# The last two groups of an attention pooling: second buffers, an interleaved order, and unread matmuls

## Chip, core and metric

The kernel runs on one core of a Trainium2 chip. The metric is device time in microseconds (us): the median over several runs of one program. The core's engines work side by side, each through its own queue of instructions in order: TensorE (PE in the profile; its weight loads, PEld, are a row of their own), VectorE (DVE), ScalarE (ACT), GpSimd (POOL) and SyncE (SP), which here only issues DMAs. TensorE writes into PSUM, eight banks of 128 x 512 float32, and the other engines read from there.

## The reference, cut to what matters

The input x has 64 sequences of 64 tokens with 256 features (4096 tokens). Two residual blocks follow each other: a linear attention with a rotated input, and a pooling that feeds a feed-forward network (FFN) with quantized operands.

```python
x = x + attn(cond(x, delta_t, amplitudes, frequencies), W_qkv, W_o, log_gamma)
x = x + ffn(cond2(x, W1, b1, v, prompt_type_ids), clip_x, clip_down, w_gate, w_up, w_down)

def cond2(hidden, W1, b1, v, ids):             # the pooling
    attn_in = jnp.tanh(jnp.einsum('bsd,da->bsa', hidden, W1) + b1)
    scores = jnp.einsum('bsa,a->bs', attn_in, v)
    ...                                        # a mask per prompt type
    p = jax.nn.softmax(jnp.where(mask, scores[:, None, :], NEG_INF), axis=-1)
    cnt = jnp.sum(mask, axis=-1).astype(hidden.dtype)
    return jnp.einsum('bjl,bld->bjd', p, hidden) / cnt[..., None]

def act_fake_quant(x, clip_factor):            # inside ffn, on its input and on h
    scale = jax.nn.sigmoid(clip_factor) * jnp.max(jnp.abs(x)) / 127.0
    return jnp.clip(round(x / scale), -128.0, 127.0) * scale

# ffn: h = silu(xq @ gate.T) * (xq @ up.T), quantized again, times down
```

What matters for the change: the scale of the FFN's input is one number, from the largest absolute value of the whole pooled tensor. No token can be quantized, and no matmul of the FFN can start, before the last group of tokens is pooled.

## The kernel before, in words

**Tiling.** The 4096 tokens are cut into eight groups (g = 0 to 7) of 512: four tiles (GT) of 128 tokens on the 128 partitions, so a tile holds two sequences. x stays in SBUF as xg[g]. `u` names a pair of tiles (256 tokens); `both` is (0, 1), `u0` is (0,) and `u1` is (1,).

**Stages.** A loop (L848 to L899) lays three groups over each other: keys, queries and values of group p, attention of group a = p - 1, pooling of group q = p - 2. The tail (L902 to L959) ends attention of group 7 (`a`) and pooling of group 6 (`q`) and 7; `a` is taken in its two halves u0 and u1. Then comes the FFN: quantizing, gate and up in four passes of 1024 tokens, a second maximum, and the down projection with the output.

**Order.** In the attention part TensorE, ScalarE, VectorE and GpSimd each run their instructions in the order in which the Python code calls them (`manual_schedule`, L120). In the FFN that holds for ScalarE, VectorE and GpSimd; TensorE's order there is laid by the planner.

**The steps of the pooling**, in the order in which a group goes through them:
- `hidden` (L437): matmuls by W1 into a bank `pa`, then on ScalarE the tanh into the tile `th` (L453).
- `token_scores` (L456): the matmul of th by v into a bank `psr` (L459).
- `softmax_exp` (L462): VectorE adds the mask to psr and writes `ms` (L470), takes the maximum (L477) and subtracts it (L478); ScalarE applies exp (L481). For group 6 the subtraction is GpSimd's.
- `softmax_div` (L483): sum (L488), product with the count (L491), reciprocal (L492), product with ms (L493, for group 6 on GpSimd).
- `weights_transposed` (L497): TensorE transposes ms into a bank `pp` (L503); ScalarE (`by_act`, L507) or VectorE (L509) copies it into the tile `pT`.
- `pooling` (L512): small matmuls of 64 x 64 from pT and x into two banks `pl` (L526): 64 instructions in the trace for a group, 32 for a half.
- `pooled_copies` (L535): ScalarE copies the two banks into `pooled` (L539).
- `pooled_maxima` (L541): VectorE reduces the same two banks (`from_banks`) to columns of `xam` (L546). The program orders two engines that touch one PSUM bank as they are written: in the tail each reduction waits for ScalarE's copy of its bank.

**What follows the pooling.** `warm` (L956) applies Silu to one column, so that its activation table is loaded before the FFN; the profile shows an ACT_TABLE_LOAD there. `act_scale` (L97) reduces xam (L100), transposes the result through the bank `pmx` (L103), reduces again (L104), and forms the scale and its inverse rx (L105, L108). `quantize_tokens` of groups 0 and 1 (L1001 on ScalarE, L999 and L1002 on VectorE) makes the first `xq`, in four pieces (two halves of the features, two groups). In `gate_up`, TensorE's first gate tile pg needs all four (L1049); among the matmuls of pg and pu in the planner's order, its last is the eighth. ScalarE then applies Silu (gate, L1060), copies pu for GpSimd (L1066) and makes the next int8 tokens (L1011).

**Buffers.** A tile of a pool with `bufs=1` is one place in SBUF: its next writer waits until the last reader of the previous tile is done. `th`, `ms` and `pT` are such tiles; the pool's default is two (L112). In PSUM `bank` (L140) takes the next of four banks of the ring `ps`, or, while `spare[0]` is set, of the ring `ps_sc`, also four, which the attention's scores use before. A bank, too, is given again only when its readers are done.

The tail is written out by hand; from L927 on, the calls are these:

```python
residual(a, 1); softmax_div(q, by=nc.gpsimd); transposed_pair(a, 1)
hidden(a, u0); hidden(a, u1); token_scores(a, u0); token_scores(a, u1)
spare[0] = True
weights_transposed(q, by_act=True); pooling(q)
spare[0] = False
...
```

Of the kernel before, what the change touches and what calls it, by code (L numbers as in the profile page):

```python
# [9 lines left out]
F32 = mybir.dt.float32  # L10
# [8 lines left out]
P = 128  # L19
# [8 lines left out]
def adaln_attn_ffn(  # L28
# [20 lines left out]
    nc = tc.nc  # L49
    B, S, D = x.shape  # L50
# [7 lines left out]
    GT = 4  # L58
# [13 lines left out]
    xg = [  # L72
        const.tile([P, GT, D], F32, tag=f"x{g}", name=f"x{g}") for g in range(NG)
    ]
# [16 lines left out]
    wgT = const.tile([P, 2, FF], BF16, name="wgT")  # L91
# [5 lines left out]
    def act_scale(cols, k, scale, inv, pt):  # L97

        mx = const.tile([P, 1], F32, name=f"mx{k}")
        nc.vector.tensor_reduce(mx, cols, AX.X, ALU.max)  # L100

        allmx = const.tile([P, 1], F32, name=f"allmx{k}")
        nc.tensor.transpose(pt, mx.to_broadcast([P, P]), ident)  # L103
        nc.vector.tensor_reduce(allmx, pt, AX.X, ALU.max)  # L104
        nc.vector.tensor_scalar(  # L105
            scale, allmx, csig[:, k : k + 1], 1.0 / QMAX, ALU.mult, ALU.mult
        )
        nc.vector.reciprocal(inv, scale)  # L108


    with ExitStack() as actx:
        pool = actx.enter_context(tc.tile_pool(name="att", bufs=2))  # L112
# [22 lines left out]
        xam = big.tile([P, 2 * NG + 2], F32, name="xam")  # L135


        spare = [False]

        def bank(name):  # L140
            if spare[0]:
                t = ps_sc.tile([P, 2, 2, 2 * S], F32, tag="sc", name=name)
                return t.rearrange("p i f c -> p (i f c)")
            return ps.tile([P, 512], F32, tag="bank", name=name)


        T = {}
# [284 lines left out]
        both = (0, 1)  # L432
# [4 lines left out]
        def hidden(g, us=both):  # L437

            pu, _ = span(us)
            pa = bank(f"pa_{g}_{us[0]}")[:, 0 : len(us) * P]  # L440
            x2v = T.pop(("x2T", g, us)).rearrange("p c (u k l) -> p c k u l", k=2, l=P)
            for kc in range(2):
                for k in range(2):
                    nc.tensor.matmul(  # L444
                        pa[k * A : (k + 1) * A, :],
                        w1s[:, kc, :],
                        x2v[:, kc, k, pu],
                        start=(kc == 0),
                        stop=(kc == 1),
                    )  # L450
            th = pool.tile([P, 2 * P], F32, tag="th", name=f"th_{g}_{us[0]}", bufs=1)
            th = th[:, 0 : len(us) * P]
            nc.scalar.activation(th, pa, AF.Tanh, bias=b1s)  # L453
            T["th", g, us] = th

        def token_scores(g, us=both):  # L456

            psr = bank(f"psr_{g}_{us[0]}")[:, 0 : len(us) * P]
            nc.tensor.matmul(psr, vb, T.pop(("th", g, us)), start=True, stop=True)  # L459
            T["psr", g, us] = psr  # L460

        def softmax_exp(g, us=both, by=nc.vector):  # L462
            _, pt = span(us)
            n = 2 * len(us)
            ms = T.get(("ms", g))
            if ms is None:
                ms = pool.tile([P, GT, S], F32, tag="ms", name=f"ms_{g}", bufs=1)
                T["ms", g] = ms
            ms = ms[:, pt]
            nc.vector.tensor_tensor(  # L470
                ms,
                T.pop(("psr", g, us)).rearrange("p (t l) -> p t l", l=S),
                T["bias", g][:, pt],
                ALU.add,
            )
            mx = pool.tile([P, GT], F32, tag="mx", name=f"mx_{g}_{us[0]}")[:, 0:n]
            nc.vector.tensor_reduce(mx, ms, AX.X, ALU.max)  # L477
            by.tensor_tensor(  # L478
                ms, ms, mx.unsqueeze(2).to_broadcast([P, n, S]), ALU.subtract
            )  # L480
            nc.scalar.activation(ms, ms, AF.Exp)  # L481

        def softmax_div(g, us=both, by=nc.vector):  # L483
            _, pt = span(us)
            n = 2 * len(us)
            ms = T["ms", g][:, pt]
            ssum = pool.tile([P, GT], F32, tag="ssum", name=f"ssum_{g}_{us[0]}")[:, 0:n]
            nc.vector.tensor_reduce(ssum, ms, AX.X, ALU.add)  # L488
            rs = pool.tile([P, GT], F32, tag="rs", name=f"rs_{g}_{us[0]}")[:, 0:n]
            c = g * GT + 2 * us[0]  # L490
            nc.vector.tensor_mul(rs, ssum, cnt[:, c : c + n])  # L491
            nc.vector.reciprocal(rs, rs)  # L492
            by.tensor_tensor(  # L493
                ms, ms, rs.unsqueeze(2).to_broadcast([P, n, S]), ALU.mult
            )

        def weights_transposed(g, us=both, by_act=False):  # L497

            _, pt = span(us)
            pp = bank(f"pp_{g}_{us[0]}")[:, 0 : len(us) * P]  # L500
            msv = T["ms", g].rearrange("p (u k) l -> p u (k l)", k=2)
            for i, u in enumerate(us):
                nc.tensor.transpose(pp[:, i * P : (i + 1) * P], msv[:, u, :], ident)  # L503
            pT = pool.tile([P, GT, S], F32, tag="pT", name=f"pT_{g}_{us[0]}", bufs=1)
            pTv = pT[:, pt].rearrange("p t j -> p (t j)")
            if by_act:
                nc.scalar.copy(pTv, pp)  # L507
            else:
                nc.vector.tensor_copy(pTv, pp)  # L509
            T["pT", g, us] = pT  # L510

        def pooling(g, us=both):  # L512

            xs, pT = xg[g], T.pop(("pT", g, us))
            _, pt = span(us)
            pls = [
                bank(f"pl_{g}_{us[0]}_{k}").rearrange("p (c t j) -> p c t j", c=2, j=S)
                for k in range(2)
            ]
            for kc in range(2):  # L520
                for t in range(2 * us[0], 2 * us[-1] + 2):
                    for dh in range(2):
                        cols = slice(kc * P + dh * 64, kc * P + (dh + 1) * 64)
                        for k in range(2):
                            half = slice(k * S, (k + 1) * S)
                            nc.tensor.matmul(  # L526
                                pls[k][dh * 64 : (dh + 1) * 64, kc, t, :],
                                xs[half, t, cols],
                                pT[half, t, :],
                                start=True,  # L530
                                stop=True,
                            )
            T["pl", g, us] = pls

        def pooled_copies(g, us=both):  # L535
            pls, pt = T["pl", g, us], span(us)[1]
            pv = pooled[g].rearrange("p c (t k j) -> p c t k j", k=2, j=S)
            for k in range(2):
                nc.scalar.copy(pv[:, :, pt, k, :], pls[k][:, :, pt])  # L539

        def pooled_maxima(g, us=both, from_banks=False):  # L541
            pls, pt = T.pop(("pl", g, us)), span(us)[1]
            pv = pooled[g].rearrange("p c (t k j) -> p c t k j", k=2, j=S)
            for k in range(2):
                col = 2 * g + k if us[0] == 0 else 2 * NG + k
                nc.vector.tensor_reduce(  # L546
                    xam[:, col : col + 1],
                    pls[k][:, :, pt] if from_banks else pv[:, :, pt, k, :],
                    AX.XYZ,
                    ALU.max,  # L550
                    apply_absolute_value=True,
                )
# [349 lines left out]
        a, q = NG - 1, NG - 2  # L902
# [27 lines left out]
        hidden(a, u0)  # L930
        hidden(a, u1)
        token_scores(a, u0)
        token_scores(a, u1)
        spare[0] = True
        weights_transposed(q, by_act=True)
        pooling(q)
        spare[0] = False
        softmax_exp(a, u0)
        softmax_exp(a, u1)
        softmax_div(a, u0)  # L940
        pooled_copies(q)
        weights_transposed(a, u0, by_act=True)
        softmax_div(a, u1)
        weights_transposed(a, u1)
        pooled_maxima(q, from_banks=True)
        pooling(a, u0)
        spare[0] = True
        pooling(a, u1)
        pooled_copies(a, u0)
        pooled_maxima(a, u0, from_banks=True)  # L950
        pooled_copies(a, u1)
        pooled_maxima(a, u1, from_banks=True)
        spare[0] = False

        warm = const.tile([P, 1], F32, name="warm")
        nc.scalar.activation(warm, hm[:, 0:1], AF.Silu)  # L956
        sx = const.tile([P, 1], F32, name="sx")
        rx = const.tile([P, 1], F32, name="rx")
        act_scale(xam, 0, sx, rx, bank("pmx_0")[:, 0:P])  # L959


    with ExitStack() as fctx:
# [234 lines left out]
```

## Time and profile before

| | us |
|---|---|
| median of 3 runs | 325.21 (324.16 to 326.14) |
| the profiled execution | 324.3 |
| its span, first to last instruction | 322.6 |
| busy: PE, DVE, ACT, POOL | 277.9, 233.3, 197.7, 87.9 |
| mean granted TensorE clock, share of full | 0.963 |

The profile is of one execution. Its times count from the start of the span. "Busy" is the time in which an engine has an instruction under way; the granted clock is the share of full speed that the chip gives to TensorE. The stages around the change in that execution:

| us from the start | what happens |
|---|---|
| 217.7 to 220.9 | last attention output matmuls (po, L399) |
| 220.7 to 224.2 | x of group 7 transposed, hidden, first token scores |
| 224.9 to 226.9 | weights of group 6 transposed and copied, group 6 pooled |
| 225.4 to 229.0 | softmax of group 7 on VectorE, both halves |
| 228.3 to 231.8 | weights of group 7 transposed and copied, group 7 pooled |
| 230.5 to 233.1 | six maxima on VectorE |
| 233.1 to 234.6 | the scale of the FFN's input |
| 234.7 to 237.5 | first tokens quantized |
| 235.8 to 283.4 | gate and up matmuls |
| 289.2 on | quantizing of h and the down projection; its matmuls begin at 290.6 |

How it is read: an engine's share of the span says little here, since each stage has another limit. The useful views are the chain of waits that ended last, the timeline of the stretch, and the table of busy time and clock by stretches.

### The profile page before, as it was taken

The page shows a single profiled execution, that of the slowest core. Times are in us where ns is not written, and L with a number is a line of the kernel's source. Part 1 is how long each engine was busy: PE and PEld are TensorE (multiplying, and loading weights), DVE is VectorE, ACT ScalarE, POOL GpSimd, SP SyncE. Part 2 cuts the span into 40 slices and gives each one's busy share as a digit, 9 for nine tenths or more (in the row PEclk, how much of TensorE's full clock was granted, in tenths as well). Part 3 has the DMA queues.
Part 4 walks back from the last instruction along what each step waited for, and adds up shares of the span by engine and source line. Part 5 has one row for each costly group of instructions (what it writes and reads, how often), then busy time and mean ns, then how long its engine had stood idle before and what let it go on. Part 6 is the DMA issues. An engine that isn't in the chain of part 4 may idle for free.

```text
span 322.6 us, 8705 instructions
## 1 busy us (share of the span) xinstructions
PE 277.9 (86%) x3762; PEld 196.9 (61%) x3766; DVE 233.3 (72%) x503; ACT 197.7 (61%) x300; POOL 87.9 (27%) x81
## 2 busy tenths in 40 slices
PE   0499999999989999999999999998478999819990
PEld 0286768758848857865875885876323433307880
DVE  6679785876997696597397378374737889977881
ACT  1566448586774755647358457363549998829930
POOL 0051240510140060045002100053008888602540
PEclk9999999999999999999999999999759999966997
DMA  5592620101100200200100010020000000000998
GB/s 150 137 327 64 207 82 20 50 2 35 35 0 2 69 2 0 69 2 4 44 25 2 13 56 2 2 70 0 3 2 0 1 0 2 0 0 0 160 192 170
DMA packets 16789, 16.15 MB, mean 50 GB/s; under 512 B 2160, under 2 KB 16496, under 8 KB 16752
## 3 DMA queue, kind: packets, MB, share of 16 engines
q1 hardware_dynamic: 12480, 11.83, 11.7%
q0 software_dynamic: 3696, 3.67, 7.5%
q8 instruction: 29, 0.48, 0.6%
q10 hardware_dynamic: 576, 0.11, 0.2%
q14 instruction: 8, 0.07, 0.1%
HBM read 7.74 MB, written 7.86 MB: 48 GB/s over the span
## 4 chain that ended last, share of the span: by engine, by line
PE 56%; DVE 22%; ACT 13%; issue 3%; DMA 3%; ACTq 0%; DVEq 0%
PE pv L215 9%; PE po L399 9%; PE pdn L1127 7%; PE pk L215 5%; PE psc L330 5%; PE py L372 4%; ACT gate L1060 4%; DVE hT L1069 3%; ACT L245 3%; DVE at L355 3%; DMA afb<-n_L_cond_amplitudes_dram 3%; PE pa L444 3%; PE pl L526 2%; PE pkT L277 2%; DVE xam L546 2%
## 5 line engine op out<-in xcount | busy, mean ns | idle before, releaser
L355 DVE TENSOR_TENSOR at<-psc,gam 128x512 f32<-128x512 f32 x62 | 38.4, 681 | 13.6 <-PE psc L330 13.6
L161 POOL TENSOR_TENSOR ys<-x,cs 128x1024 f32<-128x1024 f32 x7 | 13.8, 1968 | 110.8 <-DVE xr L175 88.9
L1067 POOL TENSOR_TENSOR hT<-gate,up 128x1024 f32<-128x1024 f32 x11 | 26.0, 2360 | 27.2 <-ACT up L1066 27.2
L399 PE MATMUL po<-woT,yT 128*128 128x256 f32 x128 | 30.7, 384 | 2.7 <-DVE kn L261 2.7
L1049 PE MATMUL pg<-xq,wgT 128*128 128x512 bf16 (+1 forms) x94 | 26.3, 397 | 4.3 <-ACT gate L1060 2.0
L215 PE MATMUL pv<-wvT,xT 128*128 128x256 f32 x128 | 29.8, 386 | 0.1
L290 PE MATMUL pq<-xT,wqT 128*128 128x512 f32 x64 | 29.5, 604 | 0.0
L215 PE MATMUL pk<-wkT,xT 128*128 128x256 f32 x128 | 29.2, 381 | 0.2 <-ACT xT L205 0.2
L1060 ACT ACTIVATE gate<-pg,wsx 128x1024 f32<-128x1024 f32 (+1 forms) x25 | 24.5, 1024 | 6.3 <-PE pg L1049 3.8
L399 PEld LDWEIGHTS po<-woT,yT 128*128 128x128 f32 x128 | 23.3, 190 | 8.2 <-DVE kn L261 5.1
L1024 DVE TENSOR_REDUCE ham<-hT 128x1 f32<-128x1024 f32 (+1 forms) x25 | 26.0, 1082 | 0.7 <-POOL hT L1067 0.7
L215 PEld LDWEIGHTS pv<-wvT,xT 128*128 128x128 f32 x128 | 23.7, 190 | 4.6 <-issue 1.4
L215 PEld LDWEIGHTS pk<-wkT,xT 128*128 128x128 f32 x128 | 23.5, 190 | 3.7 <-ACT xT L205 0.9
L1049 PE MATMUL pu<-xq,wuT 128*128 128x512 bf16 (+1 forms) x94 | 24.0, 391 | 1.6 <-DVE hT L1069 1.4
L1127 PE MATMUL pdn<-wdT,hq 128*128 128x256 bf16 x192 | 23.3, 289 | 2.3 <-DVE hq L1002 2.3
L1001 ACT ACTIVATE hq<-hT,rh 128x2560 int16<-128x2560 f32 (+4 forms) x10 | 20.1, 2095 | 6.3 <-DVE rh L108 6.3
L1127 PEld LDWEIGHTS <-hq 128*128 128x128 bf16 x192 | 19.9, 104 | 5.8 <-issue 2.6
L298 ACT ACTIVATE qbd<-pq,hm 128x512 f32<-128x512 f32 x32 | 20.1, 679 | 4.9 <-PE pq L290 4.8
L1069 DVE SCALAR_TENSOR_TENSOR hT<-pu,wsx,gate 128x1024 f32<-128x1024 f32 (+1 forms) x14 | 14.5, 1051 | 9.9 <-ACT gate L1060 9.9
L330 PE MATMUL psc<-qbd,kT 32*64 32x128 f32 x1024 | 20.2, 279 | 0.5 <-ACT kT L280 0.3
L290 PEld LDWEIGHTS pq<-xT,wqT 128*128 128x128 f32 x64 | 11.5, 190 | 14.0 <-issue 11.5
L388 ACT ACTIVATE yT<-py,hm 128x256 f32<-128x256 f32 x32 | 13.4, 470 | 10.8 <-PE py L372 10.8
(190 smaller groups left out, 524.6 us busy)
## 6 DMA issues: line engine op xcount, KB each, us to landing
x<-in_x_dram SPq DMA_DIRECT2D x8, 512.0 KB, 6.4
out_dram<-x SPq DMA_DIRECT2D x7, 512.0 KB, 3.9
out_dram<-x POOLq DMA_DIRECT2D x7, 512.0 KB, 7.6
wq_nat<-in_L_attn_W_qkv_dram SPq DMA_DIRECT2D x3, 256.0 KB, 8.7
wnat_d<-in_L_ffn_w_down_dram SPq DMA_DIRECT2D x1, 704.0 KB, 6.1
wnat<-in_L_ffn_w_gate_dram SPq DMA_DIRECT2D x1, 640.0 KB, 4.5
wnat<-in_L_ffn_w_up_dram SPq DMA_DIRECT2D x1, 640.0 KB, 5.7
out_dram<-x SPq DMA_DIRECT2D x2, 256.0 KB, 6.3
```

The source lines that it names most:

```text
L215: nc.tensor.matmul(pk[:, i * D : (i + 1) * D], xT[:, kc, t * P : (t + 1) * P], w[:, kc, :], start=(kc == 0), stop=(kc == 1),)
L290: nc.tensor.matmul(pq, wqT[:, kc, hf * P : (hf + 1) * P], xT[:, kc, :], start=(kc == 0), stop=(kc == 1),)
L298: nc.scalar.activation(qbd[:, hf, :, k, :], pq.rearrange("p (b s) -> p b s", s=S), AF.Copy, scale=hm[:, k : k + 1],)
L330: nc.tensor.matmul(banks[p][k * S : (k + 1) * S, i, hf, :], kT[rows, hf, b * S : (b + 1) * S], qbd[rows, hf, b].rearrange("p k t -> p (k t)"),
L355: nc.vector.tensor_tensor(dst, scores, by, ALU.mult)
L399: nc.tensor.matmul(po[:, i * D : (i + 1) * D], yT[:, i, hf].rearrange("p k t -> p (k t)"), woT[:, hf, :], start=(hf == 0), stop=(hf == 1),)
L1024: nc.vector.tensor_reduce(ham[:, nham : nham + 1], h, AX.XY, ALU.max, apply_absolute_value=True)
L1049: nc.tensor.matmul(dst[:, k, :] if wide else dst[k * LAST : (k + 1) * LAST, 0, :], w[:, kc, c * P : min((c + 1) * P, FF)], xq[:, kc, g * G ...
L1060: nc.scalar.activation(gate[:, ns], pg[:, ns], AF.Silu, scale=wsx[:, 0, c : c + 1])
L1067: nc.gpsimd.tensor_tensor(h, gate, up, ALU.mult)
L1069: nc.vector.scalar_tensor_tensor(h, pu[:, ns], wsx[:, 1, c : c + 1], gate[:, ns], ALU.mult, ALU.mult)
L1127: nc.tensor.matmul(pdn[:, i, :], hq[j][:, NF if last else 2 * c + k, tok], wdT[:, c + k if last else c, :], start=(c == 0), stop=(c == NC ...
```

## The change

It touches the buffers of three tiles, four helpers and the tail's order:
- `th`, `ms` and `pT` have two buffers each.
- A new helper `busy(dst, n)` issues n matmuls of the gate weights by themselves (128 x 512, bf16) into a bank that nothing reads. It is called with 3 after the pooling of group 6, with 4 after the pooling of group 7, and with 6 after the transpose in `act_scale`.
- `pooling` can do the two halves of the features (kcs) one at a time, and `pooled_copies` the two banks (ks).
- In the tail, the transposes of group 6's weights stand between the two halves' token scores of group 7; the copies of group 6 and the pooling of group 7's first half are cut in two and interleaved with the transposes; the second half's weights are copied by ScalarE and not by VectorE; the maxima of group 6 stand before the last pooling; the Silu activation `warm` stands before group 7's copies and not behind its maxima. Some banks come from the other ring.

```diff
+    def busy(dst, n):
+
+        for _ in range(n):
+            nc.tensor.matmul(
+                dst, wgT[:, 0, 0:P], wgT[:, 0, 0 : dst.shape[-1]], start=True, stop=True
+            )
...
-            th = pool.tile([P, 2 * P], F32, tag="th", name=f"th_{g}_{us[0]}", bufs=1)
+            th = pool.tile([P, 2 * P], F32, tag="th", name=f"th_{g}_{us[0]}")
...
-                ms = pool.tile([P, GT, S], F32, tag="ms", name=f"ms_{g}", bufs=1)
+                ms = pool.tile([P, GT, S], F32, tag="ms", name=f"ms_{g}")
...
-            pT = pool.tile([P, GT, S], F32, tag="pT", name=f"pT_{g}_{us[0]}", bufs=1)
+            pT = pool.tile([P, GT, S], F32, tag="pT", name=f"pT_{g}_{us[0]}")
...
-        def pooling(g, us=both):
+        def pooling(g, us=both, kcs=(0, 1)):
...
-            for kc in range(2):
+            if 0 in kcs:
+                T["pl", g, us] = [
+                    bank(f"pl_{g}_{us[0]}_{k}").rearrange("p (c t j) -> p c t j", c=2, j=S)
+                    for k in range(2)
+                ]
+            pls = T["pl", g, us]
+            for kc in kcs:
...
-        def pooled_copies(g, us=both):
+        def pooled_copies(g, us=both, ks=(0, 1)):
             pls, pt = T["pl", g, us], span(us)[1]
             pv = pooled[g].rearrange("p c (t k j) -> p c t k j", k=2, j=S)
-            for k in range(2):
+            for k in ks:
                 nc.scalar.copy(pv[:, :, pt, k, :], pls[k][:, :, pt])
...
         token_scores(a, u0)
+        spare[0] = True
+        weights_transposed(q, by_act=True)
+        spare[0] = False
         token_scores(a, u1)
         spare[0] = True
-        weights_transposed(q, by_act=True)
         pooling(q)
         spare[0] = False
         softmax_exp(a, u0)
         softmax_exp(a, u1)
+        busy(bank("idle_q"), 3)
         softmax_div(a, u0)
-        pooled_copies(q)
+        pooled_copies(q, ks=(0,))
+        spare[0] = True
         weights_transposed(a, u0, by_act=True)
+        spare[0] = False
         softmax_div(a, u1)
-        weights_transposed(a, u1)
+        pooling(a, u0, (0,))
+        pooled_copies(q, ks=(1,))
+        spare[0] = True
+        weights_transposed(a, u1, by_act=True)
+        spare[0] = False
+        pooling(a, u0, (1,))
         pooled_maxima(q, from_banks=True)
-        pooling(a, u0)
-        spare[0] = True
         pooling(a, u1)
-        pooled_copies(a, u0)
-        pooled_maxima(a, u0, from_banks=True)
-        pooled_copies(a, u1)
-        pooled_maxima(a, u1, from_banks=True)
-        spare[0] = False

         warm = const.tile([P, 1], F32, name="warm")
         nc.scalar.activation(warm, hm[:, 0:1], AF.Silu)
+        for us in (u0, u1):
+            pooled_copies(a, us)
+            pooled_maxima(a, us, from_banks=True)
+        spare[0] = True
+        pmx0, idle = bank("pmx_0")[:, 0:P], bank("idle_a")
+        spare[0] = False
+        busy(idle, 4)
         sx = const.tile([P, 1], F32, name="sx")
         rx = const.tile([P, 1], F32, name="rx")
-        act_scale(xam, 0, sx, rx, bank("pmx_0")[:, 0:P])
+        act_scale(xam, 0, sx, rx, pmx0)
+        busy(idle, 6)
```

## The prediction

> **What bounds the kernel now.** The page comes first: it says whether one engine bounds the whole or several stages have limits of their own. Its section 2 (40 slices of 8.07 us) shows a kernel that TensorE fills until slice 28. There PE and its granted clock fall together, while no other engine fills up:
>
> ```profile
> PE   0499999999989999999999999998478999819990
> ...
> ACT  1566448586774755647358457363549998829930
> ...
> PEclk9999999999999999999999999999759999966997
> ```
>
> Slices 28 and 29 (225.8 to 241.9 us) are the end of pooling and the start of gate/up: the place of the change. The chain of waits there says whose end counts: VectorE's softmax of the last group, its copy of the weights, six maxima, the scale, then eight gate/up matmuls, then ScalarE's first gate.
>
> ```profile
> 225.42 0.30 DVE ms L470
> ...
> 229.19 0.30 PE pp L503
> 229.48 0.69 PE pl L526 x32
> ...
> 230.27 0.29 DVE pT L509
> 230.56 2.53 DVE xam L546 x6
> ...
> 233.12 0.18 DVE mx L100
> ...
> 239.47 1.11 ACT gate L1060
> ```
>
> From that gate on ScalarE runs without a gap to 248.7 us, so what is gained before 239.47 is gained at the end. The timeline names each hold (start, duration, instruction; in brackets the idle time before it and what ended it):
>
> ```profile
> 224.18 0.37 ACT L453 ACTIVATE th<-pa,b1s 128x128 f32<-128x128 f32 x1 [0.78 <-PE psr L459]
> ...
> 225.42 0.29 DVE L470 TENSOR_TENSOR ms<-psr,bias 128x128 f32<-128x128 f32 x1 [3.06 <-PE pp L503]
> ...
> 227.45 1.05 ACT L539 COPY pooled_b<-pl 128x512 f32<-128x512 f32 x2
> ...
> 230.27 0.29 DVE L509 COPY pT<-pp 128x128 f32<-128x128 f32 x1 [1.23 <-PE pl L526]
> ...
> 231.80 0.65 ACT L539 COPY pooled_b<-pl 128x256 f32<-128x256 f32 x2 [0.99 <-PE pl L526]
> ...
> 232.46 1.28 ACT L956 ACT_TABLE_LOAD   x1
> ...
> 233.35 0.47 PE L103 MATMUL pmx<-ident,mx 128*128 128x128 f32 x1 [1.60 <-DVE mx L100]
> ...
> 235.79 0.61 PE L1049 MATMUL pg<-xq,wgT 128*128 128x512 bf16 x1 [1.97 <-DVE xq L1002]
> ```
>
> Three holds are single buffers: the second tanh waits until the first is read (L453), the last group's scores until the group before is transposed out of the same ms (L470), the second weights until the first pooling has read pT (L509). Last, TensorE's busy time and clock by stretch. I laid the stretches back from 230.31, where the granted clock falls, in the 3.41 us that divides the distances between its turns (230.31, 240.55, 284.96, 295.2: 10.24 is three, 54.65 sixteen):
>
> ```profile
> 223.48:226.90 3.42, 2.50 (x76) 1.79 (x71) 1.36 (x5) 1.05 (x3) 0.00 (x0) 1.00 0.00 0
> 226.90:230.31 3.41, 1.26 (x38) 0.83 (x34) 1.96 (x10) 1.69 (x5) 0.00 (x0) 1.00 0.02 5
> 230.31:233.72 3.41, 1.50 (x33) 1.12 (x33) 2.95 (x8) 2.40 (x5) 0.00 (x0) 0.50 0.01 2
> ...
> 237.14:240.55 3.41, 3.41 (x10) 1.21 (x9) 0.39 (x2) 1.08 (x2) 0.00 (x0) 0.50 0.02 5
> ```
>
> The second number is PE's busy time, the third from the end the clock. After a stretch with 1.26 of 3.41 us busy (37%) the clock is halved; after one with 2.50 (73%) it was not. At half clock gate/up matmuls start 0.427 us apart (236.62, 237.04, 237.47), later 0.216.
>
> **The change, step by step.**
>
> *Second ms, th.* Scores of the first half end at 224.15 (L453's release at 224.18), so VectorE adds the mask at 224.19 instead of 225.42: -1.23. The second half's scores must be there by 225.04, when VectorE comes to them. The second tanh no longer waits: its input ends at 223.73, it ends at 224.15. The moved transposes of group 6 run in the 0.33 to 0.71 us after the first scores' start at 223.66 (their distance now: 224.60 to 224.93 and 225.31), to 224.37; the second scores then take 224.2 to 224.74. In time. VectorE's fourteen small softmax steps follow one another without a stop now (225.42 to 229.04), so the whole stretch moves by 1.23 and ends at 227.81.
>
> *ScalarE's queue in the new order.* Group 6's weights 224.41 to 224.78, its pooling on PE (1.16) to 225.99. Exponentials to 226.32. First copy of group 6 (0.57) to 226.87. First half's weights: transposed 227.04 to 227.34 (0.15 and 0.30 behind the division, as now), copied 227.43 to 227.70. Second copy of group 6 to 228.24. Second half's weights, now by ScalarE into a second pT, transposed to 228.35, copied to 228.67. PE's last pooling (0.69 for 32 at full clock) ends at 229.41. The 1.23 that VectorE waited at L509 is gone, and VectorE takes group 6's two maxima (0.60 apart) from 227.84 to 229.12.
>
> *The moved table load.* This is the step that takes most of it back. The Silu activation now stands ahead of group 7's four copies: 1.28 of load and 0.20, from 228.68 to 230.18. The four copies (0.37 each, 0.27 apart as at 230.16) end at 230.55, 230.82, 231.1 and 231.37. Each maximum of group 7 waits for the copy of its bank, as it does now; VectorE, free at 229.12, stands still until 230.59. Four maxima 0.33 apart, the last 0.42, end at 232.00; the reduction of xam starts at 232.03 instead of 233.12: **-1.09**. Without that wait it would be 230.47 (-2.65).
>
> By the Trainium skill (ScalarE: Activation LUTs, Rules for kernel authors) a switch of tables is to be budgeted at about 2.7 us, which would put the maxima some 1.2 us later and leave nothing of the -1.09. The trace has the load at 1.28 us, the next instruction 0.02 us behind it, and the copy before it ending 0.01 us ahead.
>
> *Unread matmuls.* 128x512 bf16, 0.216 apart at full clock. Three after group 6's pooling: done by 226.6, before PE is next wanted at 227.04. Four after the last pooling: 229.41 to about 230.3, before the maximum's transpose at 232.26. Six behind that transpose: to 233.9; the first gate/up matmul is not ready before 234.54. Cover 0.4, 1.9 and 0.6 us: cost nothing. At half clock the six take 2.56 and would hold the gate matmuls by 0.6.
>
> *What a full clock is worth.* The transpose of the maximum: 0.30 (like pp) in place of 0.47: **-0.16**. Quantizing then starts at 233.44 (234.69 - 1.25). The gate's last matmul of the first eight ran from 238.75 to 239.38; its last input (the last L1002, 237.09 + 0.29) was there at 237.38, so at full clock it would have ended at 237.38 + 0.05 + 0.38 = 237.81: **-1.57**. Gate at 236.65 instead of 239.47.
>
> *At nothing.* Second buffers in the loop over groups: the waits there are of other kinds; only the tail's instructions show such a wait. Reading th, ms, pT at other addresses: no row prices it; from the spread of equal forms (0.415 to 0.416 for maxima) I take 0, +-0.1. The halves of group 6's copies and group 7's pooling: same instructions in another order. No DMA is moved.
>
> *Sum:* 1.09 + 0.16 + 1.57 = **-2.82 us**. The profiled execution took 324.3 (span 322.6): 321.5, span 319.8. Against the median 325.21: **322.4**.
>
> *Unknown: does the clock hold?* PE is idle from 230.3 to 232.26. A stretch of 3.41 us holds, by where it begins, 1.45 to 1.64 us of work at the worst (42 to 48%). Between the rows 37% (fell) and 73% (held), it is nearer to the one that fell; but much of that one was short 64-wide matmuls in small pieces, and here it is dense 512-wide ones. I take that it holds, with little lead. If it falls, by the beat of this trace at 233.72, the gate matmuls start at 234.54, 0.427 apart, until 237.14, and the eighth ends at 237.7: gate 237.8, -1.67. If it falls at 232.4, the six take half clock to 235.1, the clock is back at 235.8, gate 237.4: -2.07.
>
> The Trainium skill (TensorE: Matmul & The Clock Gate, the table on why this matters) asks only that no idle gap between bursts exceeds about 3 us. By that rule the clock holds here, with -2.82. The trace does not agree with it: the clock fell at 230.31 with no idle gap over 1.4 us in the stretch before.
>
> **The rivals.**
>
> *A, forecast:* 322.4. Chance 0.45.
>
> *B, the clock falls in the new gap:* 325.21 - 1.67 to - 2.07, 323.3. For it: 42% is close to 37%. Against: above. 0.33.
>
> *C, the other side: the transposes of group 6 block TensorE's queue.* Moved ahead of the second scores, they wait for GpSimd's division L493. Its row ends at 223.11, but spans on POOL are rough, and today's transposes prove it done only by 224.82. From 224.2 on it decides. At 224.9 the second scores come at 225.74 and VectorE's second half at 225.78 (+0.74), second weights at 229.4, maxima at 232.7 (-0.33 in place of -1.09); the gap on PE makes the clock fall, the six unread matmuls hold the gate by 0.6, and all eight at half clock put it at 239.76: +0.3, 325.5. Against it: no wait of PE for POOL in the list of waits. 0.06.
>
> *D, the maxima don't wait for the copies:* -2.65 - 0.16 - 1.57 = -4.4, 320.8. No maximum in the trace begins before the copy of its bank ends, though VectorE was busy anyway. 0.05.
>
> *E, the load holds ScalarE longer than its row.* The widest bound is all the time from the last copy to the quantizing, 232.45 to 234.69: 2.24 for 1.50. Then xam is at 232.77, the clock falls, the unread six run into the gate: 238.6 to 239.7, 325.21 - 0.9 to + 0.2, 324.8. 0.06. The table rule above is of this kind.
>
> *F, the change does not do what it says:* the freed waits return as others at the same places: 325.2. 0.05.
>
> **The numbers.** This kernel's runs (324.16 to 326.14) tell no change within about 0.5%, 1.6 us. A is faster beyond that but for noise (0.93), B in 0.6, D surely, C, E and F mostly neither: faster 0.68, same 0.26, slower 0.06. The second fall of the clock, before the down projection (4.6 us at half clock, 290.6 to 295.2), meets the beat elsewhere after a shift: 2.3 us lost now, between 1.4 and 3.4 then, so -0.9 to +1.1 on any case. Range: A and B with that, from 322.4 - 1.4 to 323.3 + 1.9, reaching C and E: 321.0 to 325.2.
>
> **What would show it.** L470 of group 7 at about 224.2 with no wait for pp; L509 gone; the table load at about 228.7, directly ahead of four copies; an idle VectorE of some 1.4 us ahead of the first 128x256 maximum, ended by ScalarE; reduction at 232.0; clock 1.00 through 240, gate matmuls 0.216 apart, first gate at 236.7. I am wrong if the maxima run on without that gap (D), if the clock is 0.5 at the first gate matmul (B), or if PE waits for POOL at L503 (C).

## The result, and the profile after

| | before | changed |
|---|---|---|
| median (range), us | 324.76 (324.16 to 326.14), 4 runs | 321.57 (320.23 to 322.07), 4 runs |
| ratio, 95% interval | | 0.9889 (0.9844 to 0.9935) |
| span of the profiled execution | 322.6 | 320.2 |
| mean granted clock | 0.963 | 0.98 |

A later series of both on another occasion gave 321.48 for 325.36, ratio 0.9891 (0.9869 to 0.9914).

The same rows of the page, for the changed kernel (slices of 8.0 us, counted from 0): PE shows 8 at slice 28, where it had 4, and still 7 at slice 29; its clock is full through slice 34.

```profile
PE   0399999999999999998999999999878999919990
...
PEclk9999999999999999999999999999999999976998
```

Two profiled executions do not begin alike: the changed one reaches the tail 0.94 us later (the chain of the changed one begins with the load of another small tensor, 9.44 us for 8.51). I therefore count from the start of the last attention residual (second x<-po,x: 220.93 before, 221.87 after) to the start of the first gate, and call this **the stretch**. It is 239.47 - 220.93 = 18.54 us before and 237.69 - 221.87 = **15.82** after: -2.72.

The chain of waits of the changed kernel in the stretch (start, duration, instruction):

```profile
225.18 0.30 DVE ms L477
...
229.51 0.27 ACT pT L514
...
229.79 1.28 ACT L967
...
231.29 0.27 ACT pooled_b L547
...
231.58 1.43 DVE xam L554 x4
233.03 0.18 DVE mx L100
...
233.26 0.34 PE pmx L103
...
237.69 1.11 ACT gate L1079
```

In these traces only ScalarE and VectorE read PSUM banks, and the chain passes through both now: from the second half's weights (L514) into the table load (L967), the copies (L547), all on ScalarE, and only then the four maxima on VectorE. Before, it stayed on VectorE from the mask addition to xam, but for the transposes and the pooling. The timeline of the same moments:

```profile
225.18 0.29 DVE L477 TENSOR_TENSOR ms<-psr,bias 128x128 f32<-128x128 f32 x1 [1.89 <-PE psr L466]
...
228.86 1.28 DVE L554 TENSOR_REDUCE xam<-pl 128x1 f32<-128x512 f32 x2
...
229.79 1.28 ACT L967 ACT_TABLE_LOAD   x1
...
231.08 0.20 ACT L967 ACTIVATE warm<-hm 128x1 f32<-128x1 f32 x1
...
231.58 1.42 DVE L554 TENSOR_REDUCE xam<-pl 128x1 f32<-128x256 f32 x4 [1.43 <-ACT pooled_b L547]
...
233.26 0.32 PE L103 MATMUL pmx<-ident,mx 128*128 128x128 f32 x1 [1.77 <-DVE mx L100]
...
235.58 0.39 PE L1068 MATMUL pg<-xq,wgT 128*128 128x512 bf16 x1 [0.70 <-DVE xq L1021]
```

The mask addition waits for its scores (psr) and no longer for the transposes of the group before (pp). VectorE does the maxima of group 6 and then stands still for 1.43 us, released by ScalarE's copy. TensorE, too, waits 0.70 us for tokens ahead of the first gate matmul: the six unread matmuls were done. Its busy time (second number) and clock (third from the end), in stretches of the same 3.41 us, laid back from the next fall of the clock at 283.44:

```profile
228.83:232.24 3.41, 2.64 (x69) 1.52 (x67) 1.98 (x5) 3.00 (x8) 0.00 (x0) 1.00 0.01 2
232.24:235.66 3.42, 1.70 (x8) 0.73 (x9) 2.03 (x9) 1.31 (x3) 0.00 (x0) 1.00 0.02 5
```

The clock held after 1.70 us of work in 3.41. The same kernel, run once more (e9 below), shows nearly the least work that such a stretch can hold here: its gap of 1.77 us lay whole within one stretch, which leaves 1.64 us of work, and the clock held there too.

```profile
230.28:233.69 3.41, 1.64 (x8) 0.64 (x7) 2.26 (x8) 1.31 (x5) 0.00 (x0) 1.00 0.02 5
233.69:237.10 3.41, 2.71 (x13) 1.18 (x13) 2.02 (x7) 1.53 (x3) 0.00 (x0) 1.00 0.00 0
```

### The profile page after: what moved, and what is told of

The parts are those of the page before. It is cut to its first block, busy times and chain, and to the rows that moved or that the text cites. A ratio compares the mean times of both kernels' runs of the same rounds, so it can differ in the third digit from the quotient of the medians.

```text
span 320.2 us, 8727 instructions
## 1 busy us (share of the span) xinstructions
PE 279.4 (87%) x3779; PEld 197.8 (62%) x3779; DVE 232.9 (73%) x502; ACT 197.7 (62%) x301; POOL 87.5 (27%) x81
## 4 chain that ended last, share of the span: by engine, by line
PE 56%; DVE 21%; ACT 14%; DMA 3%; issue 3%; ACTq 1%; DVEq 0%
PE pv L222 9%; PE po L406 9%; PE pdn L1146 7%; PE pk L222 6%; PE psc L337 5%; PE py L379 4%; ACT gate L1079 4%; DMA lgb<-in_L_attn_log_gamma_dram 3%; DVE hT L1088 3%; ACT L252 3%; DVE at L362 3%; PE pa L451 3%; PE pl L535 2%; ACT x L1030 2%; PE pkT L284 2%
## 5 line engine op out<-in xcount | busy, mean ns | idle before, releaser
L1068 PE MATMUL pg<-xq,wgT 128*128 128x512 bf16 (+1 forms) x96 | 25.1, 381 | 3.4 <-ACT gate L1079 2.7
L238 ACT ACTIVATE sq<-pk 128x512 f32<-128x512 f32 x16 | 9.6, 597 | 17.1 <-PE pk L222 17.1
```

What stands on the lines that cost most here:

```text
L1068: nc.tensor.matmul(dst[:, k, :] if wide else dst[k * LAST : (k + 1) * LAST, 0, :], w[:, kc, c * P : min((c + 1) * P, FF)], xq[:, kc, g * G ...
```

## The experiments

All stretches are from one profiled execution each; over thirteen profiles the time from the first gate to the last output sum on VectorE stays within 74.9 to 75.4 us, so a difference in the stretch goes through to that sum. Medians lie beside runs of the kernel before in the same series. The gain of a median differs from that of its stretch by -0.3 us (e1) to +1.3 us (e7), so one stretch tells a median to about 1 us and no better.

| run | stretch, us | xam reduced, us into it | median, us (before) | ratio, 95% |
|---|---|---|---|---|
| before | 18.54 | 12.19 | | |
| changed | 15.82 | 11.16 | 321.57 (324.76) | 0.9844 to 0.9935 |
| e1 no unread matmuls | 17.55 | 11.17 | 324.61 (325.28) | 0.9954 to 0.9998 |
| e2 table load last | 14.55 | 9.90 | 320.33 (325.28) | 0.9819 to 0.9878 |
| e3 maxima first | 14.29 | 9.63 | 320.88 (325.28) | 0.983 to 0.989 |
| e4 buffers only | 16.72 | 10.40 | 323.11 (325.28) | 0.9905 to 0.9959 |
| e5 unread matmuls only | 16.80 | 12.17 | 323.70 (325.49) | 0.9919 to 0.9964 |
| e8 buffers and unread, old order | 15.06 | 10.40 | 321.64 (325.49) | 0.9837 to 0.9913 |
| e6 twelve instead of six | 15.83 | 11.17 | one run, 323.21 | |
| e7 without the four | 17.85 | 11.16 | 323.52 (325.49) | 0.9913 to 0.9961 |

**e1: are the unread matmuls what holds the clock?**

```diff
-        busy(bank("idle_q"), 3)
...
-        busy(idle, 4)
...
-        busy(idle, 6)
```

> The changed kernel without its thirteen unread matmuls; all else as there. Read on the stretch from the start of the last attention residual (x, second one) to the first gate: 18.54 us before, 15.82 after. Theory (they hold the clock): the reduction of xam starts where it does now (11.2 us into the stretch), but of the 3.41 us in which it is transposed only some 0.4 us are busy, so the granted clock falls to 0.5 ahead of the first gate/up matmul, these come 0.427 us apart, and the gate is some 1.6 us later: stretch about 17.4, time about 323.2. Rival (the clock held because the new order leaves TensorE no long gap): clock 1.00 at the first gate matmul without them, stretch 15.8, time 321.6.

Stretch 17.55, 1.73 longer, and xam is reduced at the same place (11.17). The clock falls at 232.18 and is back at 239.0. Its timeline:

```profile
232.92 0.48 PE L103 MATMUL pmx<-ident,mx 128*128 128x128 f32 x1 [2.74 <-DVE mx L100]
...
237.08 1.06 PE L1065 MATMUL pg<-xq,wgT 128*128 128x512 bf16 x2
...
239.08 1.12 ACT L1076 ACTIVATE gate<-pg,wsx 128x1024 f32<-128x1024 f32 x1 [3.46 <-PE pg L1065]
```

The maximum's transpose takes 0.48 again and two gate matmuls 1.06, as before the change. The rival, that the new order alone holds the clock, is out. The median is a miss, 1.4 above the 323.2 expected: its ten executions have mean clocks of 0.960 to 0.970, and the profiled one is among the two highest; what the others lost, no profile shows.

**e2 and e3: does the early table load take part of the gain back?** e2 moves the load behind copies and maxima; e3 leaves it and lets the maxima read the banks first.

```diff
-        warm = const.tile([P, 1], F32, name="warm")
-        nc.scalar.activation(warm, hm[:, 0:1], AF.Silu)
         for us in (u0, u1):
             pooled_copies(a, us)
             pooled_maxima(a, us, from_banks=True)
+        warm = const.tile([P, 1], F32, name="warm")
+        nc.scalar.activation(warm, hm[:, 0:1], AF.Silu)
```

> The changed kernel with the Silu activation, and so its table load, put back behind the copies and maxima of the last group. Theory (the load ahead of the copies holds the maxima): VectorE's 1.43 us of waiting ahead of the first 128x256 maximum shrinks to about 0.2, the reduction of xam comes 1.2 us sooner, the load runs behind the copies in time that ScalarE has free; stretch about 14.6, time about 320.4. Rival (the load is hidden where it is, the maxima wait for the last pooling): stretch 15.8 and time 321.6, or later if the load now holds the first quantizing.

```diff
-            pls, pt = T.pop(("pl", g, us)), span(us)[1]
+            pls, pt = T["pl", g, us], span(us)[1]
...
         for us in (u0, u1):
-            pooled_copies(a, us)
             pooled_maxima(a, us, from_banks=True)
+        for us in (u0, u1):
+            pooled_copies(a, us)
```

> The changed kernel with the load left where it is, and the last group's four maxima written ahead of its four copies, so that the copies wait for the maxima. Theory (it is the order of the two readers of a bank that makes the load count): the maxima follow those of the group before with at most 0.2 us of waiting, xam is reduced 1.4 to 1.5 us sooner, the copies end before the scale is known; stretch about 14.3, time about 320.1. Rival (the maxima wait for something else than the copies): stretch 15.8, time 321.6.

Stretches 14.55 and 14.29: 1.27 and 1.53 shorter than the change, for the expected 1.2 and 1.4 to 1.5. In e2 the load ends at 231.80 and `warm` at 232.01, ahead of the inverse scale that ScalarE needs next (232.37). The timeline of e3:

```profile
228.77 2.61 DVE L554 TENSOR_REDUCE xam<-pl 128x1 f32<-128x512 f32 x6
...
229.70 1.28 ACT L967 ACT_TABLE_LOAD   x1
...
231.11 1.18 ACT L547 COPY pooled_b<-pl 128x256 f32<-128x256 f32 x4
...
231.41 0.17 DVE L100 TENSOR_REDUCE mx<-xam 128x1 f32<-128x18 f32 x1
```

Six maxima in one go, while the same load runs at the same place; the copies end at 232.29, ahead of the inverse scale (232.74). The load costs only because the maxima stand behind copies that stand behind it. Both versions are faster than the kernel before and, in the stretch, than the change.

**e4, e5, e8: the parts by themselves**, added to the kernel before.

```diff
# e4 and e8
-            th = pool.tile([P, 2 * P], F32, tag="th", name=f"th_{g}_{us[0]}", bufs=1)
+            th = pool.tile([P, 2 * P], F32, tag="th", name=f"th_{g}_{us[0]}")
...
# e5 and e8
         softmax_exp(a, u1)
+        busy(bank("idle_q"), 3)
...
         pooled_maxima(a, u1, from_banks=True)
+        idle = bank("idle_a")
         spare[0] = False
+        busy(idle, 4)
...
         act_scale(xam, 0, sx, rx, bank("pmx_0")[:, 0:P])
+        busy(idle, 6)
```

> The kernel before with second buffers for th, ms and pT and nothing else: old order, no unread matmuls, load behind the copies. Theory (the buffers give the early start, the order and the load take a part back, the unread matmuls give the clock): first mask addition of the last group 1.2 us sooner, the wait ahead of the second weights' copy down from 1.23 to about 0.5, xam reduced 1.8 us sooner than before (more than the whole change's 1.0), clock 0.5 at the gate matmuls; stretch 16.7, time about 323.0. Rival (the buffers alone free nothing, since the old order makes the same instructions wait for others): stretch 18.5, time 324.8.

> The kernel before with the thirteen unread matmuls alone (three after the pooling of the group next to last, four after the last pooling, six behind the maximum's transpose): single buffers, old order. Theory (they are worth the clock and no more): xam is reduced where it was, 12.2 us into the stretch, the clock is 1.00 at the first gate matmul, the transpose of the maximum takes 0.32 instead of 0.47, and the gate is 1.7 us sooner: stretch 16.8 for 18.54, time about 323.3. Rival (without the new order TensorE has longer gaps, which thirteen matmuls don't fill): the clock still falls, the six then take 2.56 us and hold the first gate matmuls by about 0.6: stretch 18.5 to 19.2.

> The kernel before with the second buffers and the unread matmuls, in the old order with the table load behind the last copies. Theory (the three parts add up: buffers 1.82, unread 1.73, the new order with its early load a loss of 0.83): stretch 15.0, shorter than the whole change's 15.82; time about 321.0. Rival (the new order is what lets buffers and unread matmuls work together): stretch at least 15.8.

e4 gives 16.72 (16.7 expected), e5 16.80 (16.8), e8 15.06 (15.0). In e4 the wait ahead of the second weights' copy is 0.48:

```profile
228.35 0.29 DVE L509 COPY pT<-pp 128x128 f32<-128x128 f32 x1 [0.48 <-PE pp L503]
```

There xam comes 1.79 us sooner than before, where the whole change brings 1.03. So the parts are: buffers -1.82, unread matmuls -1.74, and the new order with its early load +0.76 on top of both (15.82 - 15.06). The order itself, with the load out of the way, is a gain: e2 against e8, 14.55 to 15.06, -0.51.

**e6: do more unread matmuls cost?**

```diff
-        busy(idle, 6)
+        busy(idle, 12)
```

> The changed kernel with twelve unread matmuls behind the maximum's transpose instead of six. Theory (they cost nothing while they end ahead of the first tokens, and their own time beyond that): twelve end 2.6 us after the transpose, 0.4 us behind the time at which the first gate matmul is ready; part of this is made up, since the eighth waits for its tokens: first gate matmul 0.4 us later, gate 0.3 later, stretch 16.1. Rival (TensorE's queue is free for the gate matmuls anyway, the eighth's tokens decide alone): stretch 15.8.

A miss for the theory: stretch 15.83, not 16.1. But the edit changed more than the number of matmuls: the planner, which lays TensorE's order in the FFN, put the matmuls of gate and up in another order. In the change pg and pu are mixed and the last pg needed is the eighth of all; here the pg come first:

```profile
236.24 0.81 PE L1068 MATMUL pg<-xq,wgT 128*128 128x512 bf16 x3
...
237.24 0.38 PE L1068 MATMUL pg<-xq,wgT 128*128 128x512 bf16 x1 [0.19 <-DVE xq L1021]
...
237.46 1.02 PE L1068 MATMUL pu<-xq,wuT 128*128 128x512 bf16 x4
```

The last pg is the fifth (the record of the first is missing; its weights are loaded at 235.81, in the change at 235.57). It waits 0.19 us for its tokens and starts at 237.24 (237.22 in the change). The twelfth unread matmul starts at 235.81; with the first gate matmul 0.216 behind it and seven more steps of 0.216, the eighth would have started at 237.54 by this estimate, 0.32 late, as the theory has it. So e6 shows that twelve cost nothing in that order, and neither settles the theory nor shows slack beyond the 0.70 us for the order of the change. The one time of this run, 323.21, lies 1.1 above that of the changed kernel's profiled execution (322.07); 1.3 of it is behind the last output sum (8.4 us for 7.1).

**e7: how near was the clock to falling?**

```diff
-        busy(idle, 4)
```

> The changed kernel without the four unread matmuls after the last pooling; three and six stay. TensorE's gap ahead of the maximum's transpose grows from 1.8 to some 2.7 us. Theory (what counts is the busy share of a free-running stretch of 3.41 us, with a bound between 37 and 50%): the share of the stretch that holds the gap goes below 45% at most beats, the clock falls in most executions, the six at half clock hold the first gate matmul by up to 0.6 us: stretch 16.5 to 17.5 in those, 15.8 in the others. Rival (only an idle gap of a whole 3.4 us lets it fall): clock 1.00, stretch 15.8.

It fell in the profiled execution, at 232.11; the other five were not profiled. The stretches of 3.41 us, laid back from that fall:

```profile
228.70:232.11 3.41, 1.53 (x63) 1.07 (x53) 1.97 (x5) 2.99 (x8) 0.00 (x0) 1.00 0.01 2
232.11:235.53 3.42, 2.54 (x7) 1.03 (x8) 1.88 (x8) 1.18 (x2) 0.00 (x0) 0.50 0.02 5
235.53:238.94 3.41, 3.35 (x9) 1.01 (x8) 1.59 (x6) 0.15 (x1) 0.00 (x0) 0.50 0.00 0
```

TensorE's gap there is 2.74 us, 1.86 of it ahead of the fall (230.25 to 232.11), so the rival (a whole 3.4 us idle) is out. The stretch, 17.85, is longer than the 16.5 to 17.5 expected, and 0.30 longer than with no unread matmul at all (e1): the six behind the transpose ran at half clock, took 2.76 us, and the clock did not return after the stretch with 2.54 busy, only after the one with 3.35. The first gate matmul starts 14.47 us into the stretch (236.07), in e1 13.87 (235.40). The mean clock of its six executions, 0.970 to 0.974, lies below all ten listed of the changed kernel (0.975 to 0.980).

**The versions against each other** (e9: the change, e10: load last, e11: maxima first), five rounds in one series.

> The changed kernel once more, beside the two next ones on one chip. All theories: about 1.1% faster than the kernel before, stretch 15.8, VectorE's wait of 1.43 us ahead of the last maxima, clock 1.00 at the first gate matmul (the share of the stretch that holds TensorE's gap near 50%).

> The version with the table load behind the last copies again, to size it against the changed kernel in more rounds. Theory: 1.2 to 1.3 us less than the changed kernel in the same call, as its stretch is (14.55 for 15.82). Rival (the gain ahead of the gate is partly lost at the second fall of the clock, ahead of the down projection): less than 0.6 us between the medians.

> The version with the four last maxima ahead of the four last copies again. Theory: 1.4 to 1.6 us less than the changed kernel (stretch 14.3 for 15.8), and no more than 0.3 less than the version with the load behind the copies. Rival: as there, less than 0.6 us from the changed kernel.

Beside 325.36 for the kernel before: change 321.48, ratio 0.9891 (0.9869 to 0.9914); load last 320.80, 0.9858 (0.9834 to 0.9883); maxima first 320.70, 0.9853 (0.983 to 0.9876). The stretches repeat (15.82, 14.55, 14.29). The medians are only 0.7 and 0.8 apart from the change's: both theories (1.2 to 1.3 and 1.4 to 1.6) missed, and so did the rival (less than 0.6); the intervals of the ratios overlap. The gain in the stretch is shown; how much of it the medians keep is open between these.

## Why the prediction was right, point by point

**Forecast and time.** 322.4 in the median, of the case in which the clock holds; measured 321.57. The stretch was forecast 2.82 us shorter and is 2.72 shorter. The medians differ by more, 3.2 and 3.9 in the two series. That rest is not in the stretch, nor behind the gate (75.25 us to the last output sum before, 75.39 and 75.02 after). Two things bear on it. The profiles differ at the start (tail reached at 220.7 to 222.4) and after the last sum (7.1 to 8.8), by execution and not by kernel as far as thirteen of them show. And the profile of before, with a mean clock of 0.963, is not its commonest execution: of 41 listed in the later series, 20 stand at 0.958 to 0.960 (median 325.19 us), 9 at 0.954 (326.60), 10 at 0.963 to 0.964 (324.97); the changed kernel's ten all lie at 0.975 to 0.980. So the clock before may have cost some tenths more in the median than in the profile that the sum was made of. How the rest divides was not settled.

**Second buffers.** -1.23 forecast for the mask addition; 225.42 - 220.93 = 4.49 and 225.18 - 221.87 = 3.31 into the stretch: -1.18. By themselves the buffers are worth 1.82 (e4), since with the load behind the copies what they free at the second weights (L509: 0.48 of waiting for 1.23) counts as well.

**The moved table load.** This was the step on which the sum turned: -1.09 and not -2.65 at the reduction of xam. Measured -1.03 (12.19 to 11.16), with 1.43 us of standing still where 1.4 to 1.5 was worked out. e3 shows the other number: with the maxima ahead of the copies xam comes at 9.63, -2.56. Rival D is thus out for the change and shown as what it would have been.

The Trainium skill's budget of about 2.7 us for a switch of tables (ScalarE: Activation LUTs, Rules for kernel authors) is not borne out here: the load took 1.28 us and the next instruction started 0.01 to 0.02 us behind it, in every version; rival E had no place.

**Full clock.** -1.57 forecast for the gate matmuls, -0.16 for the transpose. e1, the change without the unread ones, loses 1.73 = 1.57 + 0.16; e5, they alone, gains 1.74. The eighth matmul ran as said, 0.38 long behind its last tokens.

**That the clock holds** was a guess between two rows (37% fell, 73% held), with chances of 0.45 and 0.33 for the two outcomes; that it came out the forecast way is in part luck. It held with 1.70 us of work in the stretch that has the gap (the prediction had 1.45 to 1.64 at the worst), and with 1.64 in e9. In e4 it fell with 1.69. So the bound lay between 37 and 73%, as said, but busy time alone does not place it: 48% held and 50% fell. The prediction's guess, that dense matmuls count for more than their time, fits this: e4's stretch is 64 small pooling matmuls and two transposes, that of e9 parts of seven 128x512 matmuls and one transpose. No run varied this alone, so it is not shown; that transposes count for less would fit as well. In both profiled executions of the change the clock held; the other eight have mean clocks (0.975 to 0.980) above all of e7, which speaks for it and doesn't prove it.

The rule in the Trainium skill's table (TensorE: Matmul & The Clock Gate, why this matters) that no gap beyond about 3 us is what matters gave the right outcome for the change and the wrong one for e7, which fell with a gap of 2.74 us there, and for the kernel before, which fell after a stretch with none over 1.33 us.

**Unread matmuls at nothing.** Right: 0.70 us of waiting for tokens stood behind them. At half clock they do hold the gate matmuls: in e7 the first starts 0.60 later than in e1, as had been worked out, and the gate comes 0.30 later.

**C, F.** TensorE never waited for GpSimd in the tail; the moved transposes ran at 224.91, right behind the first scores, and the second scores were there ahead of VectorE. None of the freed waits came back as another at its place.

## What to carry to other kernels

Where a program puts two readers of one bank in an order, as here, it makes one queue out of two engines: whatever is moved ahead of the first reader is moved ahead of the second as well. Before moving a table load "into idle time", follow who stands behind it on its engine and who waits for those; here the same load cost 1.3 us at one place and nothing at the other. And a change of several parts should be run part by part: here two parts carried 3.5 us and a third gave back 0.8, which the sum alone had hidden.

## What the runs showed that was not expected

The granted clock turned only on a beat of 3.41 us: in all thirteen profiles the distances between its turns are whole multiples of it (6.83, 10.24, 23.89, 47.79 us among them). What counts is how much TensorE did in such a stretch, and not a gap alone: before, the clock fell after a stretch whose longest gap was 1.33 us, and in the change it held with a gap of 1.77 us within one stretch (e9). Some shares of the stretches around the tail, each laid back from a turn of the clock in its own profile, and what followed:

```
before  226.90:230.31  1.26 of 3.41 (37%)  fell
e1      228.77:232.18  1.40 (41%)          fell
e7      228.70:232.11  1.53 (45%)          fell
e9      230.28:233.69  1.64 (48%)          held
e4      226.97:230.39  1.69 (50%)          fell
change  232.24:235.66  1.70 (50%)          held
e1      225.35:228.77  1.90 (56%)          held
```

The row of e4 in its own profile, beside those of the change shown above:

```profile
226.97:230.39 3.42, 1.69 (x66) 1.30 (x66) 2.76 (x9) 2.15 (x8) 0.00 (x0) 1.00 0.01 2
```

The rows of e9 and e4 overlap, so the share of busy time is not all that counts. The rows that fell consist of 64-wide pooling matmuls and transposes; with such work the clock held at 1.90 us (e1). With 128-wide matmuls it held not only at 1.64 and 1.70 but, among the last down-projection matmuls of the change (310.75 to 314.16), at 1.55; it fell after 1.26 of gate and up matmuls (e11, 277.38 to 280.79). So the bound lies between 1.69 and 1.90 us for the one kind of work in these profiles, and between 1.26 and 1.55 us for the other; what makes the difference, no run here isolates.

The way back asks for more: after a fall, a stretch with 2.54 of 3.41 us (74%, e7) brought no full clock, one with 2.67 did (78%, e8, 287.57 to 290.99). So unread matmuls are worth most before the fall; six of them after it only delayed what came next (e7).

The time from the first gate to the last output sum agreed within 0.5 us over thirteen profiles, although the clock's second fall came at 280.8 to 286.8 and its return at 289.7 to 295.2. The prediction had allowed 0.9 to 1.1 us for that.
